# The second layer's last feed-forward product as seven half-width block products, under a planner that prices changes of the array's shape

## The chip, the cores and the metric

The kernel runs on one core of a Trainium2 chip. The metric is the device time of one launch in microseconds (us). Five engines work side by side, each on its own queue: TensorE (PE: matrix products, with its weight loads listed apart as PEld), VectorE (DVE), ScalarE (ACT), GpSimd (POOL) and SyncE (SP, which here only issues DMAs). Products land in eight PSUM banks of 512 fp32 columns; everything else lives in SBUF, 128 partitions wide.

## The reference

64 graphs of 256 nodes with 256 features, all in fp32, pass two layers. Layer 0 is two graph-attention steps and a feed-forward block; layer 1 is relational attention of eight heads and a feed-forward block:

```python
# layer 0
h = gat(gat(x, adj, W1, a1), adj, W2, a2)            # softmax over leaky_relu(Wh1 + Wh2^T), masked by adj
h = layernorm(x + h)
x = layernorm(h + relu(h @ w_ff1 + b_ff1) @ w_ff2 + b_ff2)         # 256 -> 1024 -> 256
# layer 1
attn = softmax(q @ k^T / sqrt(32))                    # 8 heads of 32 columns
out = sum over r of (attn * (adj == r)) @ v_r         # relations
x = layernorm(x + out @ Wo + bo)
x = layernorm(x + gelu(x @ W1 + b1) @ W2 + b2)        # W2 is 1024 x 256: the product that is changed
```

## The kernel before

**Units of work.** Graphs are taken in pairs; each of the 32 pairs passes `gat_layers`, `feed_forward` stage 0 (relu), `attention` (stage 1) and `feed_forward` stage 2 (gelu). Several pairs are in flight at once, in different stages (`run(..., 4)`).

**Matmuls.** Nearly every product goes through `by_strips` (L113): a 128-column stationary operand is cut into four strips of 32 columns, each of which writes its own 32 partitions of a bank, so the array works as four column strips. A call of `by_strips` is four matmuls in the program; each fp32 matmul is two `MATMUL` records in the trace, so a call is eight records. Below, "a group" is one such call. The scores of attention (L929) are different: they contract over 32 rows and work as four row strips; the trace writes their shape 32*128 and that of the others 128*32.

**Products by seven.** First products of the feed-forward and the q, k and v products already multiply 2x2 blocks by the seven-product scheme (class `Blocks`, steps `p1` to `p7`; `Second` makes the four sums of the right-hand blocks on VectorE, L402; L435 adds the bank to what is there).

**The second feed-forward product.** `by_eight` computes it plainly: for each graph g and half of its rows j, eight groups of 256 columns accumulate in a bank. That is 32 groups a pair and layer; nothing but the activations of `ff` and a free bank is waited for, so the planner spreads these groups as filling wherever nothing else is ready. `add_rows` (L617) then adds the bank to the residual rows and sums each row with the same instruction; `layernorm` goes on with the squares on ScalarE (L645), the root on GpSimd (L650, L651) and centre and scale on VectorE (L654, L657). The function `by_seven` is in the file and is not called, for `SEVEN = ()`.

**Order.** A planner in the program sets the order of every engine's queue before anything runs: `put` registers a piece of work for VectorE, ScalarE, GpSimd or SyncE with a duration, a rank and the events it needs; the generators `yield` what the next TensorE step needs; `run` keeps a clock for each engine, always serves the engine that can begin first, picks TensorE's step by `degree` (lowest first, then the oldest pair) among those ready for `SLACK` us, and other engines' pieces by rank. `free` counts the buffers (`x` and `adj` four, `ff` four blocks that only one pair may hold, PSUM banks eight). `alone` lets one pair at a time into each of "gat", "ff" and "attention". `keep_order` fixes the order found.

**Other names used below.** `transposed` turns rows on VectorE (`yb`, L678), stores them and gathers them back by DMA (`home`, `yT`); on five occasions at the head and tail (`hurried`) TensorE transposes instead (L709), with four strips of 32 columns and 128 moving columns. In attention `weight` takes the exponentials (L938), `mask` multiplies (`m`, L942), `halves` adds (`h`, L946), `products` multiplies with the values (L960, L963), `into_rows` with `Wo`. In the graph attention L551 scales the rows.

Of the kernel before, what the change touches and what calls it, by code (L numbers as in the profile page):

```python
# [15 lines left out]
ALU = mybir.AluOpType  # L16
# [11 lines left out]
SEVEN = ()  # L28
SLACK = 0.3
# [4 lines left out]
def two_layers(ctx: ExitStack, tc: tile.TileContext, t: dict, out: bass.AP, flag: bass.AP):  # L34
# [114 lines left out]
    alone, filling = {}, []  # L149
# [81 lines left out]
    def run(besides, ways, together):  # L231

        going, ways = [[besides, *next(besides)]], iter(ways)
        together += 1
        def degree(g):
            if g[0] in filling:
                return 2
            return 0 if "ff" in (g[2] or ()) or alone.get("ff") is g[0] else 1  # L240

        together += 1
        while True:
            while len(going) < together and (way := next(ways, None)) is not None:
                going.append([way, *next(way)])
            first = []
            for engine, pieces in waiting.items():
                times = [(at, n) for n, p in enumerate(pieces) if (at := begins(p["ready"], p["needs"])) is not None]
                if times:
                    first.append((max(min(times)[0], clock[engine]), engine, times))  # L250
            times = []
            for n, (way, events, name, banks, *more) in enumerate(going):
                if all(alone.get(n) in (None, way) for n in name or ()) and all(e.time is not None for e in events):
                    at = begins(max([e.time for e in events], default=0.0), "bank" if banks else None, banks)
                    for needs in more:
                        at = None if at is None else begins(at, needs)
                    if at is not None:
                        times.append((at, n))
            if times:
                first.append((max(min(times)[0], clock["tensor"]), "tensor", times))  # L260
            if not first:
                assert not going
                return
            now, engine, times = min(first)
            able = [n for at, n in times if at <= now]
            clock[engine] = now
            if engine == "tensor":
                sure = [n for at, n in times if at <= now - SLACK]
                g = going[min(sure, key=lambda n: (going[n][0] is besides, degree(going[n]), n))
                          if sure else min(times)[1]]  # L270
                alone.update((name, g[0]) for name in g[2] or ())
                takes("bank", g[3])
                for needs in g[4:]:
                    takes(needs)
                step = next(g[0], None)
                if step is None:
                    together -= g[0] is besides
                    going.remove(g)
                else:
                    g[1:] = step  # L280
            else:
                piece = waiting[engine].pop(min(able, key=lambda n: (waiting[engine][n]["rank"], waiting[engine][n]["first"]["ready"])))
                takes(piece["needs"])
                if piece["function"] and piece["function"] != table[0]:
                    table[0] = piece["function"]
                    clock[engine] += 1.3
                piece["emit"]()
                clock[engine] += piece["us"]
                end = clock[engine] + piece["lag"]
                if piece["kb"]:  # L290
                    moved[0] = max(moved[0], clock[engine]) + piece["kb"] / 380.0
                    end = moved[0] + piece["lag"]
                frees_at(end, piece["frees"])
                happens(piece["event"], end)
            keep_order()
# [8 lines left out]
    def load(pair, at=None):  # L304
# [29 lines left out]
        def in_bytes(there):  # L334
            return put("vector", 1.35, largest, put("scalar", 1.2, small_adj, there, needs="adj", rank=2), rank=2)
# [51 lines left out]
    class Second:  # L387


        def __init__(self, b, name, *events):  # L390
            self.b, self.name, self.there, self.read = b, name, [], []
            for n in range(3):
                self.there.append(put("vector", 0.34, lambda n=n: self.add(n), *events, rank=0, needs=None if n else name))
                events = self.there[-1:]
# [9 lines left out]
        def read_by_second(self, event):  # L404
            self.read.append(event)
            if len(self.read) == 2:
                put("vector", 0.34, lambda: self.add(3), self.there[2], *self.read, rank=0, event=self.there[3])
# [7 lines left out]
    class Blocks:  # L415
# [17 lines left out]
        def add(self, c, h, bank, *events, frees=()):  # L433
            def add():
                nc.vector.tensor_tensor(self.target(c, h), self.bank[bank], self.target(c, h), ALU.add)  # L435
            there = put("vector", 0.6, add, *events, rank=-1, frees=frees)
# [41 lines left out]
    def addends(y, there, at, layer, pair):  # L478
# [20 lines left out]
        there = put("scalar", 0.6, exps, *there, rank=0, function="exp")  # L499
# [28 lines left out]
        there = put("vector", 0.2, turn, there, rank=0)  # L528
# [3 lines left out]
    def gat_weights(y, at, at_home, ratio, there, to, b):  # L532
# [20 lines left out]
        there = put("vector", 0.95, lambda: weigh(0), *there, rank=b / 2, needs="e")  # L553
        there = put("vector", 1.13, lambda: weigh(1), there, rank=b / 2, frees=["rows"] * b)
        return of, put_each("scalar", 0.4, [lambda j=j: scale(j) for j in range(2)], there, rank=0)

    def gat_layers(pair, to, loads):
# [3 lines left out]
        def evacuated(to, k, wide, ps):  # L561
            return put("scalar", 0.3, lambda: nc.scalar.activation(to[:, k, :wide], ps[:, :wide], AF.Copy),
                       took(0.88), frees=["bank"])
# [45 lines left out]
    def add_rows(y, p, b, *events):  # L609
# [12 lines left out]
        return of, put_each("vector", 0.44, [lambda j=j: add(j) for j in range(2)], *events, frees=["bank"])  # L622

    def means(y, b, *events):
# [8 lines left out]
        return of, put_each("scalar", 0.54, [lambda j=j: mean(j) for j in range(2)], *events)  # L633

    def layernorm(r, gb, b, added, *events):
# [23 lines left out]
        there = put_each("scalar", 0.54, [lambda j=j: square(j) for j in range(2)], there, rank=0)  # L659
        centred = put_each("vector", 0.34, [lambda j=j: centre(j) for j in range(2)], there)  # L660
        there = put("gpsimd", 1.2, root, there, rank=0)
        return put_each("vector", 0.34, [lambda j=j: scale(j) for j in range(2)], there, centred, *events)
# [5 lines left out]
    def transposed(y, ready, to, b, pair, stage):  # L668
# [23 lines left out]
        there = put("vector", 0.62, turn, ready, needs="yb")  # L692
# [25 lines left out]
    def feed_forward(y, normal, w, func, relieved, gb, pair, stage):  # L718
# [11 lines left out]
        def slabs(t):  # L730
# [11 lines left out]
            def copy(c, h, event):  # L742
                return put("scalar", 0.5, lambda: nc.scalar.activation(target(c, h), blocks.bank["x"], AF.Copy), event, rank=-1)  # L743

            def activate(c, h, event, of=None, frees=()):
                for n in range(2):
# [3 lines left out]
                        to, source, func, bias=b1[:, m:m + 1]), event, rank=h - 1, function=kind,  # L750
# [9 lines left out]
        for step in (a.p1, b.p1, a.p2, a.p6, b.p2, b.p6, a.p5, a.p7, b.p7, b.p5, a.p4, b.p4, a.p3):  # L760
            yield from step()
# [28 lines left out]
    def by_seven(y, normal, f, evacuated, w2, w2_there, last):  # L790
# [21 lines left out]
        def add(to, of, us, *events, frees=()):  # L812
            return put("vector", us, lambda: nc.vector.tensor_tensor(to, of, to, ALU.add), *events, rank=-1, frees=frees)

        def combine(to, a, b, op, *events):
            return put("vector", 1.14, lambda: nc.vector.tensor_tensor(to, a, b, op), *events, rank=0)
# [40 lines left out]
    def attention(y, normal, pair, all_adj):  # L857
# [13 lines left out]
        there = put("scalar", 0.52, lambda: in_one_piece(0), normal[0], needs="yTa")  # L871
        there = put("scalar", 0.52, lambda: in_one_piece(1), there, normal[1], frees=["yT"])
# [27 lines left out]
        def with_bias_qk(c, b, event, frees=()):  # L900
            def copy(n):
                nc.scalar.activation(target_qk(c, b)[:, n], of_qk.bank["x"][:, n], AF.Identity, bias=bqk[:, n, c:c + 1])  # L902
            return [put("scalar", 0.4, lambda n=n: copy(n), event, rank=-1, frees=list(frees) * n) for n in range(2)][1]

        def with_bias_v(r, b, event, frees=()):
# [3 lines left out]
            return put("vector", 0.6, copy, event, rank=-1, frees=frees)  # L909
# [11 lines left out]
        def scores(n):  # L921
            b, c = divmod(n, KC)
            yield [ready["qk", c, b]], None, HQ
# [7 lines left out]
            there = took(1.13)  # L931
# [12 lines left out]
            def halves(q):  # L944
# [3 lines left out]
            there = [put_each("scalar", 0.48, [lambda q=q, k=k: weight(q, k) for k in range(2)], there, rank=0, function="exp",  # L948
                              needs="a", frees=["bank"] * 2) for q in range(HQ // 2)]
            masked.append([put("vector", 1.14, lambda q=q: mask(q), there[q], rank=0, needs="m") for q in range(HQ // 2)] +  # L950
                          [put("vector", 0.61, lambda q=q: halves(q), there[q], rank=0, needs="h") for q in range(HQ // 2)])

        def products(n):
# [10 lines left out]
            there = took(2.34)  # L964
# [16 lines left out]
            there = put("vector", 1.3, invert, there, rank=0)  # L981
            put("scalar", 0.4, check, there, rank=3)
            return put("vector", 0.34, lambda: nc.vector.tensor_tensor(to, po[:, :N], s, ALU.mult), there, rank=0, frees=["bank", "h"])
# [10 lines left out]
        a_, b_ = of_qk, of_v  # L994
        for step in (a_.p1, b_.p1, a_.p2, a_.p6, b_.p2, a_.p5, b_.p6, a_.p7, b_.p5, a_.p4, b_.p7, a_.p3, b_.p4, lambda: scores(0), b_.p3, lambda: scores(1)):
            yield from step()
        frees_at(clock["tensor"], ["yTa", "sums_yTa"])
        divided = []
        for n in range(4):
            yield [*masked[n], ready["v", 0, n // 2], ready["v", 1, n // 2]], None, 1  # L1000
            divided.append(products(n))
            if n < 2:
                yield from scores(n + 2)
# [85 lines left out]
    def whole_way(pair):  # L1089
        to, loads = loaded.pop(pair)  # L1090
        if pair + 1 < NPAIR and pair + 1 not in loaded:
# [5 lines left out]
        put("sync", 0.4, lambda: nc.sync.dma_start(  # L1097
            out[2 * pair:2 * pair + 2].rearrange("b (c p) d -> p (b c) d", p=P), to["x"]),
            normal[0], normal[1], rank=2, lag=1.8, kb=512, frees=["x"])

    run(reliefs(), (whole_way(pair) for pair in range(NPAIR)), 4)


# [442 lines left out]
```

## Time and profile before

| | before |
|---|---|
| median of 3 runs | 3002.74 us (3000.09 to 3004.53) |
| the profiled execution: time, span of its instructions | 3002.45 us, 3000.6 us |
| mean granted TensorE clock | 0.996 |
| PE busy, PE records | 2962.5 us (99%), 53778 |
| DVE busy | 2308.1 us (77%) |
| ACT busy | 1789.2 us (60%) |
| POOL busy | 293.3 us (10%) |
| HBM | 67 GB/s over the span |

Busy times are sums over the span; a busy PE is not a PE at its peak, since the ends of its matmuls are modelled, so the spacing of starts is what tells how fast it goes. A row of the groups reads: line, engine, operation, tiles written and read with their shapes, count, then busy time, the mean ns of one instruction, and the idle time ahead of them with what ended it. In a timeline a row reads: start, length, engine and line, what it writes and reads, and how many instructions were merged; two starts that follow each other give the rate.

### The profile page before, as it was taken

The page shows a single profiled execution, that of the slowest core. Times are in us where ns is not written, and L with a number is a line of the kernel's source. Part 1 is how long each engine was busy: PE and PEld are TensorE (multiplying, and loading weights), DVE is VectorE, ACT ScalarE, POOL GpSimd, SP SyncE. Part 2 cuts the span into 40 slices and gives each one's busy share as a digit, 9 for nine tenths or more (in the row PEclk, how much of TensorE's full clock was granted, in tenths as well). Part 3 has the DMA queues.
Part 4 walks back from the last instruction along what each step waited for, and adds up shares of the span by engine and source line. Part 5 has one row for each costly group of instructions (what it writes and reads, how often), then busy time and mean ns, then how long its engine had stood idle before and what let it go on. Part 6 is the DMA issues. An engine that isn't in the chain of part 4 may idle for free. (4 is left out here: it accounts for less than half of the span.)

```text
span 3000.6 us, 122479 instructions
## 1 busy us (share of the span) xinstructions
PE 2962.5 (99%) x53778; PEld 1766.1 (59%) x53778; DVE 2308.1 (77%) x5865; ACT 1789.2 (60%) x4644; POOL 293.3 (10%) x518
## 2 busy tenths in 40 slices
PE   7999999999999999999999999999999999999998
PEld 4655555555555555555555555555556555565665
DVE  5787875888668887588976888768886788867775
ACT  4555565665656566556665566555666565664554
POOL 0000010000101011000110001101010001100001
PEclk8999999999999999999999999999999999999999
DMA  5221231112321123121231212311232121321100
GB/s 178 80 72 52 65 110 63 52 59 66 108 65 55 55 72 119 52 69 38 92 103 55 62 51 89 99 52 59 65 97 76 59 65 53 100 74 49 39 10 24
DMA packets 211420, 210.22 MB, mean 70 GB/s; under 512 B 22336, under 2 KB 170432, under 8 KB 210880
## 3 DMA queue, kind: packets, MB, share of 16 engines
q1 hardware_dynamic: 210464, 202.06, 21.2%
q8 instruction: 424, 6.95, 1.0%
q14 instruction: 116, 0.95, 0.1%
q10 hardware_dynamic: 416, 0.26, 0.0%
HBM read 137.51 MB, written 64.73 MB: 67 GB/s over the span
## 5 line engine op out<-in xcount | busy, mean ns | idle before, releaser
L113 PE MATMUL ps<-w_L_gnn_W,ff 128*32 128x256 f32 x8192 | 470.7, 380 | 1.3 <-ACT ff L749 1.3
L113 PE MATMUL ps<-w_L_gnn_w_ff,ff 128*32 128x256 f32 x8192 | 470.7, 379 | 0.0
L113 PEld LDWEIGHTS ps<-w_L_gnn_W,ff 128*32 128x32 f32 x8192 | 260.1, 110 | 186.5 <-issue 13.6
L113 PEld LDWEIGHTS ps<-w_L_gnn_w_ff,ff 128*32 128x32 f32 x8192 | 265.1, 110 | 177.5 <-issue 3.6
L938 ACT ACTIVATE a<-ps 128x512 f32<-128x512 f32 x512 | 265.5, 600 | 170.3 <-PE ps L929 153.4
L435 DVE TENSOR_TENSOR ff<-ps,ff 128x512 f32<-128x512 f32 x384 | 262.3, 684 | 118.1 <-PE ps L113 89.6
L650 POOL TENSOR_SCALAR rstd<-squares 128x2 f32<-128x2 f32 x256 | 90.8, 355 | 2679.6 <-ACT unread L645 2678.3
L645 ACT ACTIVATE unread<-x,less 128x256 f32<-128x256 f32 x512 | 259.3, 506 | 130.1 <-DVE less L620 103.7
L942 DVE TENSOR_TENSOR m<-a,adj 128x1024 f32<-128x1024 f32 x256 | 310.7, 1214 | 23.9 <-ACT a L938 23.0
L113 PE MATMUL ps<-yT,w_L_gnn_W1p 128*32 128x256 f32 x5120 | 310.0, 379 | 0.8 <-ACT ff L743 0.3
L113 PE MATMUL ps<-yT,w_L_gnn_w_ff1p 128*32 128x256 f32 x5120 | 306.7, 379 | 0.0
L617 DVE SCALAR_TENSOR_TENSOR x<-ps,x 128x256 f32<-128x256 f32 x512 | 197.3, 417 | 136.0 <-PE ps L113 133.0
L743 ACT ACTIVATE ff<-ps 128x512 f32<-128x512 f32 x384 | 224.2, 588 | 112.9 <-PE ps L113 111.3
L113 PE MATMUL ps<-xw,e 128*32 128x258 f32 (+1 forms) x4096 | 242.7, 386 | 11.9 <-ACT xw L551 11.9
L551 ACT ACTIVATE xw<-xw,rs 128x258 f32<-128x258 f32 (+1 forms) x256 | 118.0, 504 | 201.2 <-DVE rs L547 201.1
L113 PEld LDWEIGHTS ps<-yT,w_L_gnn_W1p 128*32 128x32 f32 x5120 | 165.6, 110 | 112.9 <-ACT ff L743 4.9
L113 PEld LDWEIGHTS ps<-yT,w_L_gnn_w_ff1p 128*32 128x32 f32 x5120 | 165.5, 110 | 110.9 <-issue 2.3
L902 ACT ACTIVATE qk<-ps,bqk 128x256 f32<-128x256 f32 x256 | 107.1, 469 | 190.0 <-PE ps L113 189.8
L749 ACT ACTIVATE ff<-ff,c_L_gnn_b_ff 128x256 f32<-128x256 f32 x384 | 175.5, 503 | 50.5 <-DVE ff L435 47.8
L651 POOL TENSOR_TENSOR rstd<-rstd,mhalf 128x2 f32<-128x2 f32 x256 | 201.8, 788 | 21.3
L113 PEld LDWEIGHTS ps<-xw,e 128*32 128x32 f32 x4096 | 133.8, 112 | 104.6 <-ACT xw L551 14.1
L749 ACT ACTIVATE ff<-ff,c_L_gnn_b 128x256 f32<-128x256 f32 x384 | 175.9, 502 | 28.6 <-DVE ff L435 26.0
(126 smaller groups left out, 4748.2 us busy)
## 6 DMA issues: line engine op xcount, KB each, us to landing
home<-yb SPq DMA_DIRECT2D x182, 256.0 KB, 2.1
yT<-home SPq DMA_DIRECT2D x728, 64.0 KB, 2.1
rows<-row SPq DMA_DIRECT2D x60, 512.0 KB, 3.9
input<-in_xT SPq DMA_DIRECT2D x32, 512.0 KB, 4.0
x<-in_x SPq DMA_DIRECT2D x32, 512.0 KB, 3.9
out<-x SPq DMA_DIRECT2D x32, 512.0 KB, 3.0
input<-in_adjT SPq DMA_DIRECT2D x30, 512.0 KB, 4.0
v<-in_adjT SPq DMA_DIRECT2D x2, 512.0 KB, 7.5
```

What stands on the lines that cost most here:

```text
L113: nc.tensor.matmul(to[at:at + DH], lhsT=lhsT[:, at:at + DH], rhs=rhs, **flags)
L435: nc.vector.tensor_tensor(self.target(c, h), self.bank[bank], self.target(c, h), ALU.add)
L551: nc.scalar.activation(y[:, k, :at], y[:, k, :at], AF.Copy, scale=of["rs"][:, j:j + 1])
L617: nc.vector.scalar_tensor_tensor(row, p[:, j * D:(j + 1) * D], 1.0, row, op0=ALU.mult, op1=ALU.add, accum_out=of["less"][:, j:j + 1])
L645: nc.scalar.activation(unread, rows[j], AF.Square, bias=of["less"][:, j:j + 1], accum_out=squares[:, j:j + 1])
L650: nc.gpsimd.tensor_scalar(rstd, squares, 1.0 / D, EPS, ALU.mult, ALU.add)
L651: nc.gpsimd.tensor_tensor(rstd, rstd, mhalf[:, :2], ALU.pow)
L743: return put("scalar", 0.5, lambda: nc.scalar.activation(target(c, h), blocks.bank["x"], AF.Copy), event, rank=-1)
L749: evacuated[h][m] = put("scalar", 0.4, lambda m=m, to=to, source=source: nc.scalar.activation(to, source, func, bias=b1[:, m:m + 1]), even ...
L902: nc.scalar.activation(target_qk(c, b)[:, n], of_qk.bank["x"][:, n], AF.Identity, bias=bqk[:, n, c:c + 1])
L938: nc.scalar.activation(a[n][q][:, k], ps[2 * q + k], AF.Exp)
L942: nc.vector.tensor_tensor(m[n][q], a[n][q], adj, ALU.mult)
```

## The change

1. **By seven.** `SEVEN = (2,)`: the second product of stage 2 runs through `by_seven`. W2 is loaded by `last_weights` as seven blocks of 512 x 128 (four DMAs in place of one); `last_sums` makes three of them and rewrites a fourth with four VectorE subtractions at the start. Per pair seven products of eight groups with 128 moving columns take the place of 32 groups with 256. Between them VectorE makes four block sums of the activations (`combine`, t1 to t4, 128 x 1024 each, in place) and six additions of banks to the residual rows (d1, d5, d6, d3 of 128 x 256; d24 and d7 of 128 x 512). `add_rows` falls away in this stage; the row sums come from `means`, four ScalarE passes with an accumulator (L645 after, 128 x 256 each). The product order is 4, 1, last step of the first product, 5, 6, 2, 7, 3.
2. **The planner knows shapes.** A step may be named "rows" (the scores); a change between it and the others adds 0.1 to the planner's TensorE clock, the scores' and the products' own planned durations are lowered to match, and `degree` has a place for "rows" and for a second one in a row. `GROUPS` writes out how products and scores alternate.
3. **Five pairs** may be in flight (`FLIGHT = 5`), with the same buffers.
4. **Chosen precedences.** `SLACK` is 0; ranks of all kinds of pieces stand in `RANK`, the degrees in `DEGREE`, and the orders of the steps in `FIRST` (feed-forward) and `QKV` (attention).
5. The output of a pair is stored in two halves, each as soon as its graph is ready, where one DMA stored both.

```diff
-SEVEN = ()
-SLACK = 0.3
+SEVEN = (2,)
+SHAPES = ("rows",)
+SLACK = 0
+FLIGHT = 5
+RANK = {"adj": 1.5, "second": 0.5, "blocks": 0, "exps": 1.5, "addends": 1.5, "weigh": 3, "ratios": 0, ...
+DEGREE = {"first": 0.5, "gat": 1, "attention": 1.5, "fill": 2.5, "rows": -1, "after": 2.5}
+GROUPS = (([0], []), ([], [2]), ([1], []), ([], [3]), ([2], []), ([3], []))
+FIRST = ("a1", "a2", "b1", "a6", "b6", "b2", "a7", "a5", "b7", "a3", "b4", "a4", "b5")
+QKV = ("a1", "b1", "b2", "a6", "a2", "a5", "b6", "b7", "b5", "a7", "a4", "a3", "s0", "b4", "b3", "s1")
...
-            if g[0] in filling:
-                return 2
-            return 0 if "ff" in (g[2] or ()) or alone.get("ff") is g[0] else 1
+            kind = ("fill" if g[0] in filling else "first" if "ff" in (g[2] or ()) or alone.get("ff") is g[0] else
+                    "attention" if "attention" in (g[2] or ()) or alone.get("attention") is g[0] else "gat")
+            return DEGREE["after" if shaped[0] and shape(g) else shape(g) or kind]
...
+                if shape(g) != shaped[0]:
+                    clock[engine] += 0.1
+                    shaped[0] = shape(g)
...
-        centred = put_each("vector", 0.34, [lambda j=j: centre(j) for j in range(2)], there)
+        centred = put_each("vector", 0.4, [lambda j=j: centre(j) for j in range(2)], there, rank=RANK["centre"])
...
-            there = took(1.13)
+            there = took(0.97)
...
-            there = took(2.34)
+            there = took(2.17)
...
-        for n in range(4):
-            yield [*masked[n], ready["v", 0, n // 2], ready["v", 1, n // 2]], None, 1
-            divided.append(products(n))
-            if n < 2:
-                yield from scores(n + 2)
+        for groups, later in GROUPS:
+            yield from narrow(groups, later)
...
-        put("sync", 0.4, lambda: nc.sync.dma_start(
-            out[2 * pair:2 * pair + 2].rearrange("b (c p) d -> p (b c) d", p=P), to["x"]),
-            normal[0], normal[1], rank=2, lag=1.8, kb=512, frees=["x"])
+        there = []
+        for b in range(2):
+            there.append(put("sync", 0.4, lambda b=b: nc.sync.dma_start(
+                out[2 * pair + b].rearrange("(c p) d -> p c d", p=P), to["x"][:, of_graph(b), :]),
+                normal[b], *there, rank=2, lag=1.8, kb=256, frees=["x"] * b))
-    run(reliefs(), (whole_way(pair) for pair in range(NPAIR)), 4)
+    run(reliefs(), (whole_way(pair) for pair in range(NPAIR)), FLIGHT)
```

`by_seven`, which stood in the file and is called now (`done`, `quarter` and `two_halves` pick activations, a quarter of the rows and a bank):

```python
        def product(n, to, side, first=False):
            for b in range(2):
                for k in range(half):
                    by_strips(to[:, b], lhsT=side[:, k, b * P:(b + 1) * P], rhs=w2[:, n - 1, k], ...)
            return took(1.8)
        ...
        read4 = product(4, left[:, 0], a22, True)
        t1 = combine(a22, a21, a22, ALU.add, *done(0, 0), *done(0, 1), read4)
        t3 = combine(a21, a11, a21, ALU.subtract, *done(1, 1), t1)
        yield done(1, 1), None, 1
        read1 = product(1, x, a11, True)
        d1 = add(quarter(0, 0), x, 0.34, read1)
        t2 = combine(a11, a22, a11, ALU.subtract, t3, read1)
        yield from last.p3()
        ...
        yield [t1], None, 1
        read5 = product(5, v, a22, True)
        d5 = add(quarter(1, 1), v, 0.34, read5)
        yield [t2, d1], None, 0
        d6 = add(quarter(0, 1), x, 0.34, product(6, x, a11))
        yield done(1, 0), None, 0
        read2 = product(2, left[:, 1], a12)
        d24 = add(rows[:, :, :, :P], left, 0.6, read2, read4, frees=["bank"])
        t4 = combine(a12, a12, a11, ALU.subtract, t2, read2)
        yield [t3, d6], None, 0
        d7 = add(...product(7, x, a21), d5, frees=["bank"])
        yield [t4, d5], None, 0
        d3 = add(quarter(0, 1), v, 0.34, product(3, v, a12), frees=["bank"])
        normal["added"] = [means(y, g, d24, d7, d3) for g in range(2)]
```

## The prediction

> **What bounds the kernel now.** I first read the busy times of the page, then the same by stretches of the span:
>
> ```profile
> PE 2962.5 (99%) x53778; PEld 1766.1 (59%) x53778; DVE 2308.1 (77%) x5865; ACT 1789.2 (60%) x4644; POOL 293.3 (10%) x518
> ...
> 0.00:100.00 100.00, 80.67 (x1273) 52.36 (x1276) 57.54 (x185) 46.31 (x120) 5.15 (x14) 0.90 0.49 150
> 100.00:1000.00 900.00, 894.19 (x16236) 529.63 (x16232) 709.65 (x1805) 541.47 (x1423) 89.62 (x154) 1.00 0.23 70
> 1000.00:2000.00 1000.00, 997.74 (x18180) 593.26 (x18176) 776.02 (x1979) 611.74 (x1574) 102.29 (x181) 1.00 0.23 73
> 2000.00:2950.00 950.00, 948.82 (x17316) 565.55 (x17312) 744.58 (x1842) 571.86 (x1487) 89.94 (x160) 1.00 0.19 61
> 2950.00:3000.60 50.60, 41.08 (x798) 25.31 (x786) 20.29 (x57) 17.83 (x46) 6.27 (x11) 0.95 0.08 24
> ```
>
> After the length of each stretch come PE, PEld, DVE, ACT and POOL. From 100 to 2950 us PE has nothing to do for only 5.8 + 2.3 + 1.2 = 9.3 us; the rest of its 38 idle us lie in the first 100 us (19) and the tail (9.5). VectorE is at 78% there. So the time is PE's work plus head and tail. A busy share doesn't say how fast PE is; the timeline's starts do:
>
> ```profile
> 1573.64 12.27 PE L113 MATMUL ps<-w_L_gnn_W,ff 128*32 128x256 f32 x224
> 1585.73 2.77 PE L113 MATMUL ps<-yT,w_L_gnn_w_ff1p 128*32 128x256 f32 x48
> ...
> 1637.02 2.77 PE L113 MATMUL ps<-yT,w_L_gnn_w_ff1p 128*32 128x256 f32 x48
> 1639.72 1.15 PE L929 MATMUL ps<-qk 32*128 32x256 f32 x16
> 1640.80 1.07 PE L960 MATMUL ps<-a,v 128*32 128x256 f32 x16
> 1641.68 1.05 PE L960 MATMUL ps<-m,v 128*32 128x256 f32 x16
> ...
> 2952.88 1.06 PE L709 MATMUL ps<-ident,x 128*32 128x128 f32 x32
> 2953.75 1.91 PE L113 MATMUL ps<-w_L_gnn_W,ff 128*32 128x256 f32 x32
> 2955.48 1.06 PE L709 MATMUL ps<-ident,x 128*32 128x128 f32 x32
> 2956.35 1.03 PE L113 MATMUL ps<-w_L_gnn_W,ff 128*32 128x256 f32 x13
> ```
>
> The first two rows are the product to be replaced: 224 records in 12.09 us, so a group of eight takes 0.432 us. The last four hold the shape that replaces it (strips of 32, 128 moving columns): 32 records in 0.87 us, 0.218 us a group. Half the columns cost 50.5% of the time, in bursts. The middle rows price a change of shape: 48 records start 2.70 us ahead of the scores where six groups need 2.59; the scores hold PE 1.08 us where two groups need 0.86; the next 16 take 0.88. That is 0.11 + 0.22 + 0.02 = 0.35 us for going there and back.
>
> [...] the trace lists 110 ns a load, overlapping, and can't say whether they would hold a longer run back. [...]
>
> **The change, part by part.**
>
> *PE work.* Removed per pair: 32 groups x 0.432 = 13.82 us. Added: 7 x 8 = 56 groups x 0.218 = 12.21. Saved 1.61 us, over 32 pairs **-51 us**. Bounds: the best is this; if a product of eight groups takes the planner's 1.8 instead of 1.75, 7 x 0.05 x 32 = 11 us of it are lost.
>
> *Shape changes.* In the instruction order after, the scores are still 128 separate blocks of eight, never two in a row. The 128 x 0.35 = 45 us stay: **0**. Pricing them in the plan moves steps, it removes none.
>
> *VectorE.* Rows for the prices:
>
> ```profile
> L942 DVE TENSOR_TENSOR m<-a,adj 128x1024 f32<-128x1024 f32 x256 | 310.7, 1214 | 23.9 <-ACT a L938 23.0
> L435 DVE TENSOR_TENSOR ff<-ps,ff 128x512 f32<-128x512 f32 x384 | 262.3, 684 | 118.1 <-PE ps L113 89.6 <-ACT ff L743 27.1 <-ACT unread L645 0.5
> L617 DVE SCALAR_TENSOR_TENSOR x<-ps,x 128x256 f32<-128x256 f32 x512 | 197.3, 417 | 136.0 <-PE ps L113 133.0 <-PE ps L1111 2.3
> ```
>
> Added: 128 block sums x 1.214 = 155 us, 128 small adds x 0.415 = 53, 64 wide ones x 0.684 = 44. Removed: 128 row additions x (0.417 + 0.082 for reading the accumulator) = 64, and 64 small scalings x 0.169 = 11. Net +177 us: 2308 + 177 = 2485, 84% of the forecast span. It lies beside PE, except where a product waits for it.
>
> *The wait that is new.* `by_eight` waited for nothing behind its activations; five products of `by_seven` wait for VectorE. The order after is the same for nearly 27 pairs in a row, so one walk stands for most. Zero is the end of product 4. PE: `Wo` 1.73, product 1 to 3.48, last first-product step 0.86, so product 5 starts at 4.34, 6 at 6.09, 2 at 7.83, 7 at 9.58, 3 at 11.33. VectorE's order, each at its mean less the 0.08 us by which neighbours overlap (two of 476 ns last 0.88 in the tail's timeline), from 0.2: t1 to 1.33, a centre 1.73, t3 2.86, two row additions with their small scaling 3.86, t2 5.0, d1 5.3 (product 6 wants both at 6.09: 0.8 to spare), the last `ff` addition 5.9, a sum, a centre, d5, a sum 7.3, two scales 8.1, a sum, d6 8.8 (product 7 at 9.58: 0.8 to spare), `yb` 9.4, two centres 10.2, t4 11.35; [...]. So **+0.2 us a pair, +6 us**. Bounds: 0 if VectorE enters early, about 1 us a pair (+32) if it enters late, since all behind it is shifted.
>
> *ScalarE.* `means` add 128 x (0.506 + 0.190) = 89 us. In the order after, exponentials and gelu change places twice a pair, 64 table loads where the trace counts 53 + 35 + 17 + 1 = 106; 42 x 1.283 = 54 us go. Net +35: 61%, beside PE, which is busy throughout: **0** in the middle; with that cover gone it would be at most these 35 us. GpSimd makes the same 256 roots. Attention's exponentials no longer meet as many loads, which is why I cost their re-ordering at nothing.
>
> *Five pairs, ranks, orders.* They can win back at most the 9.3 us that PE idles between 100 and 2950, and lose what a badly placed wait costs. I take **0**; bounds -9 and +10. The `x` buffers stay four, so the fifth pair can run only to the end of its graph attention. The head (19 idle us, and 10 lost in two stretches at half clock, PEclk 0.90) is bound by the first loads; its order changes in details: **0**, bounds -8 and +8. Three more weight DMAs and four subtractions lie there, far ahead of their first use; 32 more output DMAs on SP, half as large, stand behind no load that PE awaits.
>
> *Tail.* Today one graph's normalization follows the last matmul. After, both wait for d3: d3 0.4, then four means and four squares on ScalarE at 0.61, 4.9 in all, where now two row additions and two squares take 2.2. **+3 us**; the last store is half as large, so between +1 and +5.
>
> *Sum:* -51 + 6 + 3 = -42 against the profiled execution's 3002.45, so 2960.4; the median of the runs is 0.3 above that execution: **2960**.
>
> **Rivals.**
>
> *VectorE becomes the second bound* (0.15): at 84% it enters the run of products about 0.7 us late in most pairs, behind attention's `m` and `h`; 22 us more, 2980 (2978 to 2996). For it: the walk leaves t4 no room. Against: in attention the order gives all masks of a block some 0.7 us or more before its product.
>
> *Slower* (0.08): the same place, carried further. PE has no filling between products 5 and 3, which stand together as 160 matmuls in the order, so each us that VectorE arrives late is paid in full. From 1.5 us late a pair the saving is eaten, from 1.7 the kernel is slower; at 2 us 2960 + 58 = 3018. Against: ranks put the block sums ahead of everything they meet.
>
> *No gain* (0.03): the short matmuls aren't sustained. If sets of four need 123 ns instead of 109 because their weight loads fall behind, 56 x 2 x 0.123 = 13.8 us, nothing is saved. [...] against: eight sets in a row kept 109.
>
> *More* (0.05): head and idle time shrink too: 2935.
>
> **How the numbers follow.** The likeliest case, 0.69, is 2960, own range 2940 to 2978 (bounds of head, tail, product rate and stall). Range 2938 to 2990, leaving out most of the case "more", the end of the second-bound case and the slower one. A measurement can tell about 0.2% (6 us) from no change: faster 0.69 + 0.15 + 0.05 = 0.89, same 0.03, slower 0.08.
>
> **What would show it.** PE records 53778 + 6144 = 59922; new matmuls of 128 columns at 0.218 us a group (1.75 a product); scores still 1.08; DVE near 2485 us; 64 table loads; idle PE ahead of products 6, 7 and 3 with a DVE releaser, near 0.2 us a pair. Wrong, if sets take over 115 ns, if PE waits over 1 us a pair for L828 or L831 (the changed kernel's additions and block sums), or if the idle between 100 us and the tail is over 40 us.

## The result, and the profile after

The change is faster by 1.5%: 2958.09 us median (2957.19 to 2962.04, 4 runs) against 3003.23 (3000.09 to 3004.53, 4 runs, one more than in the table above), a ratio of 0.9854 with a 95% interval of 0.9839 to 0.9868. The profiled execution took 2957.19 us, its span is 2955.4. The forecast was 2960, with a range of 2938 to 2990.

The same views as before, of the changed kernel: the page's busy times, then the stretches (length, PE, PEld, DVE, ACT, POOL, granted clock, DMA share, GB/s).

```profile
PE 2915.5 (99%) x59922; PEld 1908.3 (65%) x59922; DVE 2459.3 (83%) x5869; ACT 1796.1 (61%) x4858; POOL 266.3 (9%) x518
```

```profile
0.00:100.00 100.00, 77.66 (x1192) 49.29 (x1196) 58.15 (x183) 43.63 (x114) 4.85 (x14) 0.88 0.48 150
100.00:1000.00 900.00, 898.57 (x18327) 577.29 (x18320) 764.39 (x1842) 558.78 (x1518) 81.62 (x160) 1.00 0.23 74
1000.00:2000.00 1000.00, 1000.00 (x20640) 653.39 (x20636) 847.05 (x2024) 619.00 (x1678) 91.06 (x180) 1.00 0.23 73
2000.00:2900.00 900.00, 899.05 (x18675) 596.11 (x18671) 757.35 (x1750) 550.92 (x1479) 81.67 (x153) 1.00 0.19 61
2900.00:2955.40 55.40, 40.20 (x1118) 32.23 (x1110) 32.40 (x74) 23.80 (x70) 7.12 (x12) 0.91 0.07 23
```

PE is even fuller than before, with 1.4 + 0.0 + 1.0 = 2.4 us of idle between 100 and 2900 us; what has shrunk is its work. The timeline of one pair's seven products, TensorE alone (L122 is `by_strips`, which was L113):

```profile
1508.28 1.93 PE L122 MATMUL ps<-w_L_gnn_W,ff 128*32 128x128 f32 x64
1510.03 1.91 PE L122 MATMUL ps<-w_L_gnn_Wo,qk 128*32 128x256 f32 x32
1511.75 1.93 PE L122 MATMUL ps<-w_L_gnn_W,ff 128*32 128x128 f32 x64
1513.50 1.05 PE L122 MATMUL ps<-yT,w_L_gnn_W1p 128*32 128x256 f32 x16
1514.36 9.08 PE L122 MATMUL ps<-w_L_gnn_W,ff 128*32 128x128 f32 x320
1523.26 2.77 PE L122 MATMUL ps<-yT,w_L_gnn_w_ff1p 128*32 128x256 f32 x48
```

Product 4 holds PE from 1508.28 to 1510.03, 1.75 us, and product 1 the same. Products 5, 6, 2, 7 and 3 are the 320 records from 1514.36 to 1523.26: 8.90 us where five times 1.75 is 8.75. The missing 0.15 us is a wait that PE's idle time doesn't show, since the modelled ends of the matmuls cover it. The list of waits names it, in 27 pairs of 32 (waiting engine, who was waited for, us in total, times, longest):

```profile
PEld ps L122 <- DVE ff L831: 5.8, 27, 0.2
```

VectorE's timeline in the same stretch shows the four block sums (L831) and what stands ahead of the fourth:

```profile
1510.35 1.23 DVE L831 TENSOR_TENSOR ff<-ff 128x1024 f32<-128x1024 f32 x1 [0.20 <-ACT ff L763]
...
1511.88 1.22 DVE L831 TENSOR_TENSOR ff<-ff 128x1024 f32<-128x1024 f32 x1
...
1513.90 1.22 DVE L831 TENSOR_TENSOR ff<-ff 128x1024 f32<-128x1024 f32 x1
...
1518.83 0.71 DVE L692 STREAM_TRANSPOSE yb<-x 128x512 f32<-128x512 f32 x1
1519.45 0.84 DVE L668 SCALAR_TENSOR_TENSOR x<-x,less,b_L_gnn_g 128x256 f32<-128x256 f32 x2
1520.21 1.22 DVE L831 TENSOR_TENSOR ff<-ff 128x1024 f32<-128x1024 f32 x1
```

t4 ends 11.40 us after product 4 (1521.43 less 1510.03); product 3 could have started at 1514.36 + 4 x 1.75 = 1521.36. The groups that are new (busy time, mean ns, idle time ahead), and ScalarE's new pass and most of its table loads, which in the trace stand ahead of a gelu and of an exponential in turn (five more stand at other lines, 64 in all):

```profile
L831 DVE TENSOR_TENSOR ff<-ff 128x1024 f32<-128x1024 f32 x128 | 156.1, 1220 | 10.1 <-ACT ff L763 6.1 <-PE ps L122 3.7
L828 DVE TENSOR_TENSOR x<-ps,x 128x256 f32<-128x256 f32 x128 | 53.3, 417 | 3.5 <-PE ps L122 2.7 <-PE ps L1135 0.8
L828 DVE TENSOR_TENSOR x<-ps,x 128x512 f32<-128x512 f32 x64 | 44.0, 688 | 4.1 <-PE ps L122 1.0
```

```profile
L645 ACT ACTIVATE unread<-x 128x256 f32<-128x256 f32 x128 | 53.4, 417 | 44.7 <-DVE x L828 41.9 <-DVE all_of_them L1137 0.2
L763 ACT ACT_TABLE_LOAD x32 | 41.1, 1283 | 0.6
L508 ACT ACT_TABLE_LOAD x27 | 34.6, 1283 | 0.1
```

### The profile page after: what moved, and what is told of

The parts are those of the page before. It is cut to its first block, busy times and chain, and to the rows that moved or that the text cites. A ratio compares the mean times of both kernels' runs of the same rounds, so it can differ in the third digit from the quotient of the medians.

```text
span 2955.4 us, 135318 instructions
## 1 busy us (share of the span) xinstructions
PE 2915.5 (99%) x59922; PEld 1908.3 (65%) x59922; DVE 2459.3 (83%) x5869; ACT 1796.1 (61%) x4858; POOL 266.3 (9%) x518
## 4 chain that ended last, share of the span: by engine, by line
## 5 line engine op out<-in xcount | busy, mean ns | idle before, releaser
L122 PE MATMUL ps<-w_L_gnn_w_ff,ff 128*32 128x256 f32 x8192 | 490.4, 380 | 0.0
L122 PE MATMUL ps<-w_L_gnn_W,ff 128*32 128x128 f32 x14336 | 414.5, 273 | 0.3 <-issue 0.3
L122 PEld LDWEIGHTS ps<-w_L_gnn_W,ff 128*32 128x32 f32 x14336 | 393.8, 110 | 23.3 <-DVE ff L831 5.8
L122 PEld LDWEIGHTS ps<-w_L_gnn_w_ff,ff 128*32 128x32 f32 x8192 | 259.7, 110 | 187.3 <-issue 30.2
L122 PE MATMUL ps<-yT,w_L_gnn_W1p 128*32 128x256 f32 x5120 | 307.8, 381 | 4.6 <-ACT yT L727 4.0
L122 PE MATMUL ps<-yT,w_L_gnn_w_ff1p 128*32 128x256 f32 x5120 | 306.1, 379 | 0.5 <-DVE ff L449 0.4
L664 POOL TENSOR_SCALAR rstd<-squares 128x2 f32<-128x2 f32 x256 | 61.3, 240 | 2661.7 <-ACT unread L659 2661.5
L122 PE MATMUL ps<-xw,e 128*32 128x258 f32 (+1 forms) x4096 | 245.3, 386 | 13.3 <-ACT xw L565 13.2
L122 PEld LDWEIGHTS ps<-yT,w_L_gnn_W1p 128*32 128x32 f32 x5120 | 166.1, 110 | 111.0 <-ACT yT L727 4.2
L122 PEld LDWEIGHTS ps<-yT,w_L_gnn_w_ff1p 128*32 128x32 f32 x5120 | 168.5, 110 | 103.2 <-DVE ff L449 0.9
L631 DVE SCALAR_TENSOR_TENSOR x<-ps,x 128x256 f32<-128x256 f32 x384 | 145.1, 414 | 74.7 <-PE ps L122 74.4
L665 POOL TENSOR_TENSOR rstd<-rstd,mhalf 128x2 f32<-128x2 f32 x256 | 204.3, 798 | 21.3
L122 PEld LDWEIGHTS ps<-xw,e 128*32 128x32 f32 x4096 | 136.0, 112 | 103.8 <-ACT xw L565 16.4
L960 DVE TENSOR_TENSOR h<-a 128x512 f32<-128x512 f32 x256 | 167.8, 687 | 15.3 <-ACT a L952 15.3
L122 PE MATMUL ps<-yTa,wqk 128*32 128x256 f32 x2560 | 167.2, 379 | 0.2 <-DVE qk L449 0.2
```

What stands on the lines that cost most here:

```text
L122: nc.tensor.matmul(to[at:at + DH], lhsT=lhsT[:, at:at + DH], rhs=rhs, **flags)
L631: nc.vector.scalar_tensor_tensor(row, p[:, j * D:(j + 1) * D], 1.0, row, op0=ALU.mult, op1=ALU.add, accum_out=of["less"][:, j:j + 1])
L664: nc.gpsimd.tensor_scalar(rstd, squares, 1.0 / D, EPS, ALU.mult, ALU.add)
L665: nc.gpsimd.tensor_tensor(rstd, rstd, mhalf[:, :2], ALU.pow)
L960: nc.vector.tensor_tensor(h[n][q], a[n][q][:, :, :N], a[n][q][:, :, N:], ALU.add)
```

## The experiments

In the table, "idle" is PE's idle time between 100 and 2900 us: 2800 less its busy time there, from the stretches of each run's trace. Short waits are hidden in busy time, so "lost" counts otherwise: every record of TensorE in that stretch at the start-to-start price that unbroken stretches of its shape show in the traces of before and the change (27.3 ns for 128 columns, 54.0 for 256, 54.4 and 54.8 for 258 and 260, 67.3 in the scores), taken from 2800. Some 16 us of it are changes of shape (128 times 0.13, the 0.11 and 0.02 of the timeline before; the rest of their price being in the scores' 67.3). As the prices are rounded, "lost" may be off by a few us; its differences are better.

Each ratio below is to runs of the kernel before that were made beside the experiment; their medians lie between 3003.4 and 3004.7 us. A difference to the change, whose runs were made at another time, can be off by 1 or 2 us.

| kernel | median us | idle us | lost us |
|---|---|---|---|
| before | 3003.2 | 9.3 | 31 |
| the change | 2958.1 | 2.4 | 25 |
| plain product, all else changed (e1) | 3016.9 | 21.1 | 45 |
| seven products, nothing else (e2) | 3037.1 | 55.5 | 100 |
| the change with four pairs (e3) | 3011.2 | 32.3 | 74 |
| the change without shapes (e4) | 2970.9 | 11.6 | 34 |
| one more VectorE operation ahead of t4 (e5) | 2991.7 | 34.3 | 56 |
| the same operation behind d24 (e6) | 2959.5 | 3.6 | 26 |
| product planned at 1.75 us (e7) | 2953.6 | 3.5 | 22 |
| seven products in both layers (e8) | 3008.4 | 55.8 | 126 |
| before, seven products and five pairs (e9) | 3035.7 | 58.9 | 103 |
| before, five pairs (e10) | 3026.2 | 21.3 | 46 |
| e7 with six pairs (e11) | 2968.8 | 14.3 | 38 |
| the change with the old ranks (e12) | 2999.1 | 39.0 | 71 |

### Which part of the change brings the time

**e1**, the new plan without the products:

```diff
-SEVEN = (2,)
+SEVEN = ()
```

> The changed kernel with the plain second product in both layers, so the new planner, five pairs and precedences alone. Theory (the seven products are the gain): TensorE's work is that of before again, so about 50 us more than the change less the 6 us of waits and the 3 us of tail, 2958 + 41 = 2999, within 9 us of before (2990 to 3004). Rival (the better plan brought most of it): under 2980, since the order alone would have won 25 us or more.

3016.85 us (3016.74 to 3019.99), ratio to before 1.005 (1.0033 to 1.0066). Both theories missed: the plan alone isn't neutral, it is slower than before. TensorE waits for q and k once in nearly every pair (PE's own waits):

```profile
PE ps L122 <- DVE qk L449: 16.5, 27, 1.6
```

An order that fits the changed work doesn't fit the old. An order chosen for the plain product was not looked for. In the middle it could win at most some 15 us: the 31 lost before, less the 16 of the shapes.

**e2**, the products without the new plan:

```diff
-SEVEN = ()
+SEVEN = (2,)
```

> The kernel before with the seven products in the second layer and nothing else changed. Theory (TensorE's work sets the time, the plan only has to keep up): 2955 to 2975, that is nearly the whole gain. Rival (the seven products only pay under the new plan, since under the old one TensorE waits for VectorE between them): 2985 or more, with over 20 us of TensorE idle behind VectorE's block sums and additions.

3037.13 us (3034.47 to 3038.96), ratio 1.0111 (1.0094 to 1.0128). My theory fell and the rival held. TensorE has the same work as in the change, and what it loses more than eats the gain: 100 us in the middle where it was 31 before, and some 16 us more at the tail. The longest waits of its weight loads for another engine:

```profile
PEld ps L113 <- DVE ff L816: 37.3, 34, 2.6
PEld ps L113 <- ACT ff L743: 25.1, 29, 2.2
```

One pair in its timeline, TensorE:

```profile
1462.01 3.68 PE L113 MATMUL ps<-w_L_gnn_W,ff 128*32 128x128 f32 x128
1465.50 1.05 PE L113 MATMUL ps<-yT,w_L_gnn_W1p 128*32 128x256 f32 x16
1466.66 1.95 PE L113 MATMUL ps<-w_L_gnn_W,ff 128*32 128x128 f32 x64
1470.59 5.45 PE L113 MATMUL ps<-w_L_gnn_W,ff 128*32 128x128 f32 x192 [1.97 <-DVE ff L816]
1476.23 1.96 PE L113 MATMUL ps<-w_L_gnn_W,ff 128*32 128x128 f32 x64 [0.20 <-DVE ff L816]
```

Products 4 and 1 stand together as 128 records, without the `Wo` block that lies between them in the change. So product 5 comes due 1.73 us sooner after product 4 and waits for t1; product 5 ends at 1466.66 + 1.75 = 1468.41 and product 6 starts at 1470.59, over 2 us late, behind t3 and t2. VectorE is also late to begin: t1 starts at 1465.39, 1.63 us after product 4 (1462.01 + 1.75 = 1463.76), where in the change it starts 0.32 us after it (1510.35 less 1510.03).

**e9**, the products and the fifth pair under the old precedences (`SEVEN = (2,)`, and 5 for 4 in `run`):

> The kernel before with the seven products in the second layer and five pairs in flight, all precedences as before. Theory (the seven products need both, a fifth pair and an order in which VectorE serves them in time): 2985 to 3030, with TensorE still waiting 25 us or more for VectorE ahead of the products. Rival (the fifth pair alone makes them pay, as the loss with four suggests): 2975 or less.

3035.65 us (3030.53 to 3046.24), ratio 1.0106 (1.0079 to 1.0134). The fifth pair doesn't rescue the products; the time is over the theory's range, too. The waits behind the block sums shrink to 10.7 us for the weight loads (37.3 in e2) and 6.1 for the matmuls behind them, below the 25 I expected, and others take their place: weight loads wait 38.7 us for `ff` from ScalarE (25.1 in e2).

**e10**, the fifth pair alone:

> The kernel before with five pairs in flight and nothing else. Theory (with the plain products as filling TensorE idles only 9 us in the middle, so there is nothing for a fifth pair to fill): 2994 to 3012. Rival (a fifth pair is worth as much here as in the changed kernel, where taking it away cost 53 us): under 2980.

3026.18 us (3025.64 to 3035.05), ratio 1.008 (1.006 to 1.01). Slower than either theory said: 15 us more lost in the middle, 9 at the tail, and nothing at the head.

**e3**, four pairs (`FLIGHT = 4`) in the changed kernel:

> The changed kernel with four pairs in flight. Theory (TensorE never lacks work between head and tail, a fifth pair adds nothing): 2955 to 2966. Rival (with less filling the fifth pair is what keeps TensorE supplied): 2975 or more, with idle TensorE in the middle of the span.

3011.24 us (3008.61 to 3023.92), ratio 1.0033 (1.002 to 1.0045). The rival held: 53 us lost, with 32.3 us of idle, spread over the graph attention's products (weight loads wait 32.5 us for L565), the `ff` blocks (22.2) and the masks (16.5).

**e12**, the old ranks in the changed kernel:

```diff
-RANK = {"adj": 1.5, "second": 0.5, "blocks": 0, ... "sums": -1, "qk": -2, ... "mask": 1, ... "centre": 2, ...}
+RANK = {"adj": 2, "second": 0, "blocks": -1, ... "sums": 0, "qk": -1, ... "mask": 0, ... "centre": 1, ...}
```

> The changed kernel with the ranks of all pieces as they were before (block sums of the second product and masks at 0, additions and bank copies at -1, the rest as in the kernel before); five pairs, degrees, the orders of the steps, the groups and the shape charge as changed. Theory (the ranks are what keeps VectorE and ScalarE ahead of TensorE): 2985 or more, TensorE idle over 30 us in the middle. Rival (step orders and degrees carry it, ranks are trimming): under 2972.

2999.14 us (2992.98 to 3006.6), ratio 0.9984 (0.9977 to 0.9991). The theory held: 41 us of the 45 go with the ranks alone. The wait that the change has at 0.2 us is here about 1 us in 29 pairs, seen by the weight loads (the matmuls behind them wait 19.9 us of it). It is about half of what is lost more in the middle; the rest is spread over other waits:

```profile
PEld ps L122 <- DVE ff L831: 27.7, 29, 1.3
```

**e4**, the planner without shapes (no charge, `took(1.13)` and `took(2.34)` as before, no degree for the scores):

> The changed kernel whose planner doesn't know the shape changes: no charge for them, the scores' and products' planned durations as before, the scores with no degree of their own; the rest as changed. Theory: the 128 changes of shape and their 0.35 us stay in both kernels, so it is within 10 us of the change (2952 to 2970). Rival (the pricing itself brings time): slower by 15 us or more.

2970.86 us (2969.0 to 2976.55), ratio 0.9896 (0.9879 to 0.9912). 12.8 us slower than the change, between the two theories. The scores are 128 blocks in each, and in the change's trace they still go from 1561.42 to 1562.50, 1.08 us, as before. So what the planner's better clock brings is not in the shapes; most of it is the wait for the block sums, which in the change comes to 5.8 us:

```profile
PEld ps L122 <- DVE ff L831: 17.3, 28, 1.1
```

### Where VectorE binds

**e5** and **e6** add the same operation of 1.2 us to each pair, unknown to the planner, in two places. **e5**, ahead of t4:

```diff
+    idle = const.tile([P, 4, N], F32, name="idle")
+    nc.vector.memset(idle, 0.0)
...
+        def late():
+            nc.vector.tensor_tensor(idle, idle, idle, ALU.add)
+            nc.vector.tensor_tensor(a12, a12, a11, ALU.subtract)
-        t4 = combine(a12, a12, a11, ALU.subtract, t2, read2)
+        t4 = put("vector", 1.14, late, t2, read2, rank=RANK["sums"])
```

> The changed kernel with one more VectorE operation a pair, a 128x1024 addition on a tile of its own, directly ahead of the block sum t4; the planner doesn't know of it, so every queue keeps its order. Theory (VectorE has no room left ahead of product 3, which has no filling behind it): product 3 waits 1.13 us longer in nearly every pair, 30 to 38 us more, 2988 to 2996. Rival (VectorE at 83% takes another 1.2% in its stride): under 2966.

2991.66 us (2989.04 to 2994.05), ratio 0.9961 (0.9946 to 0.9976): 33.6 us more than the change, as the theory said. TensorE shows it where it was expected, ahead of product 3 (L124 is the changed kernel's L122, L867 is t4):

```profile
1529.74 7.17 PE L124 MATMUL ps<-w_L_gnn_W,ff 128*32 128x128 f32 x256
1538.00 1.95 PE L124 MATMUL ps<-w_L_gnn_W,ff 128*32 128x128 f32 x64 [1.08 <-DVE ff L867]
```

Product 3 was due at 1529.74 + 4 x 1.75 = 1536.74 and starts 1.26 us later, where the change has 0.15. The 1.11 us between them in each of the 29 pairs that wait are 32 us.

**e6** (`idle` as in e5):

```diff
+        def both():
+            nc.vector.tensor_tensor(rows[:, :, :, :P], left, rows[:, :, :, :P], ALU.add)
+            nc.vector.tensor_tensor(idle, idle, idle, ALU.add)
-        d24 = add(rows[:, :, :, :P], left, 0.6, read2, read4, frees=["bank"])
+        d24 = put("vector", 0.6, both, read2, read4, rank=RANK["last"], frees=["bank"])
```

> The same additional operation, but two places later on VectorE, behind the addition d24, the planner again not knowing of it. Theory (it is the place and not the load that counts: no product stands behind it before VectorE has caught up): 0 to 8 us more, 2956 to 2966. Rival (VectorE is a second bound by its load): as much as with the operation ahead of t4, 25 us or more.

2959.52 us (2957.19 to 2959.97), ratio 0.9852 (0.9837 to 0.9867): nothing that these runs resolve. VectorE's busy time is the same in both (2496.6 and 2493.5 us), so it is the place and not the load: two operations further on, 32 operations of 1.2 us are free. The wait for t4 stays what it is in the change:

```profile
PEld ps L124 <- DVE ff L833: 5.8, 27, 0.2
```

**e7** sets the planner's figure to the measured one:

```diff
-            return took(1.8)
+            return took(1.75)
```

> The changed kernel with one figure of the planner set to what the trace shows: a product of eight half-width groups takes 1.75 us, not 1.8. TensorE's order in the steady stretch stays as it is; on VectorE one of the two centre operations that stood ahead of t4 falls behind it, so t4 ends 0.4 us earlier. Theory (product 3 waits about 0.2 us for t4 in 27 of 32 pairs): this wait goes, 4 to 7 us less, 2951 to 2955. Rival (the 0.2 us are a hand-over that stays whatever stands ahead): within 2 us of the change.

2953.61 us (2952.8 to 2956.63), ratio to before 0.9835 (0.9822 to 0.9848), 4.5 us better than the change; the runs of the two don't overlap, though the intervals of their ratios overlap a little. The five products go from 1512.41 to 1521.14, 8.73 us, and of the waits for L831 a single one of 0.3 us is left:

```profile
1512.41 8.92 PE L122 MATMUL ps<-w_L_gnn_W,ff 128*32 128x128 f32 x320
1521.14 2.77 PE L122 MATMUL ps<-yT,w_L_gnn_w_ff1p 128*32 128x256 f32 x48
```

This is the fastest version of the study.

**e8**, both layers (`SEVEN = (0, 2)`):

> The changed kernel with the seven products in both layers. TensorE's work falls by another 50 us, VectorE's rises by 177 to some 2640 us. Theory (no plain product is left as filling, VectorE is at 90%, and waits for it eat the gain): 2970 to 3040, over 60 us of TensorE idle more. Rival (TensorE's work still sets the time): under 2925.

3008.39 us (2997.97 to 3016.2), ratio 1.0014 (1.0006 to 1.0022). The time is in the theory's range, with 53 us more idle than the change where the theory had over 60. TensorE has 66066 records and waits most of all behind attention's masks on VectorE, which now is busy 2629.9 us (87%), and ScalarE 2034.8:

```profile
PEld ps L974 <- DVE m L956: 44.5, 49, 1.0
```

The ranks weren't chosen for this work, and the order that the planner finds here has 218 table loads of 1.28 us where the change has 64, so how much is VectorE's load and how much the order isn't told apart.

**e11**, six pairs on top of e7 (`FLIGHT = 6`):

> The changed kernel with the product's planned duration at 1.75 us, as in the run before, and six pairs in flight. Theory (TensorE idles under 4 us between head and tail, the sixth pair finds nothing to fill and the rows' buffers are four): 2950 to 2960. Rival (any other number of pairs than the one for which the precedences were chosen loses): 2970 or more, with TensorE idle in the middle.

2968.81 us (2963.93 to 2972.43), ratio 0.988 (0.9863 to 0.9896): 15 us worse than e7, just short of the rival's figure, with 14.3 us of idle, weight loads waiting 18.2 us for `ff` from ScalarE.

## Why the prediction was right, and where it wasn't

**PE work, -51: right.** A product takes 1.75 us alone, and 8.73 for five in e7, where nothing is waited for: 0.218 us a group over 320 records, as the transposes showed over 32. All records at their start-to-start prices come to 51 us less. The rival of short matmuls that can't be sustained is out: a set of four takes 109 ns in the long run, too (8.73 us over 80 sets), beside weight loads that the trace lists at 110 ns each, overlapping.

**The wait, +6: right.** The walk had product 3 due at 11.33 and t4 end at 11.35, and t4 ended at 11.40, step by step within 0.2 us of the walk. What the forecast of 0.2 us a pair held beyond these 0.02 was the author's estimate of a hand-over that no trace showed; here the first weight load of product 3 starts 0.05 us behind the end of t4 (1521.48 less 1521.43). In 30 pairs the five products stand together; beyond 8.73 us they lose 5.3 us in all, 0.16 in nearly every pair. Taking the cause away in e7 gave back 4.5 us. e5 tests the slope that the "slower" rival rested on, at one point: an operation that takes VectorE 1.13 us (from the start of t4 to that of the next in the change, 1520.21 to 1521.34) cost 1.11.

**Tail, +3: smaller where it was put, and a second part was missing.** From the end of the last product to the end of the span it was 3000.6 - 2991.07 = 9.5 us and is 2955.4 - 2944.2 = 11.2: +1.7. The prediction had all four means wait for d3; but d3 writes only one of the two blocks of rows that each graph has, and two of the means start ahead of it, at 2943.54 and 2944.08 against 2944.26. What it didn't have lies ahead of the last products: TensorE waits 4.0 us once for the last pair's transposed rows, and the 48 records behind that wait take 4.30 us in place of 2.59, at a granted clock of 0.60. Both together are +5.7.

**Head, 0: missed by 4,** within its bounds: 3 us more idle, and a granted clock of 0.88 for 0.90.

**Five pairs, ranks, orders, 0 within -9 and +10: this step failed,** though the sum didn't show it, in two ways. As a number: between 100 and 2900 us TensorE loses 6 us less than before in spite of the new waits of 5.3, so the rest has shrunk by 11. The bound was drawn from idle time alone, which leaves short waits out: weight loads waited 13.9 + 6.2 us for `ff` from ScalarE before, and 0.7 in the change. As an argument: it treated the plan as an addition to the products. The runs show that they can't be added. Against the kernel before, the products under the old plan cost 34 us, the fifth pair alone 22, both together 31, and the plan without the products 13; all of it wins 45. Taken from the whole, the ranks are worth 41 us, the fifth pair 53, the shapes 13. That the order can win back at most the idle of before could hold at best for a kernel whose products wait for nothing. Each of these settings makes the planner find another order, so the differences belong to that order and not to the setting as such; which ranks matter was not tried.

**Together** -51 + 5 + 7 + 4 - 11 = -46, where the spans differ by 45. PE's work and the wait came out as forecast, because they were walked through the order that the changed kernel really has. That the sum came within 2 us is in part luck: tail and head cost 9 us more than forecast, and the order gave 11 more.

**VectorE, +177:** the new groups took 156 + 53 + 44, as priced. The durations of all its instructions add up to 185 us more; the busy time rose by only 151, since the page counts overlapping neighbours once. **ScalarE, +35:** 64 table loads, as forecast. The pass of `means` was mis-sized: 417 ns and not the 506 of the squares, so 128 x (0.417 + 0.187) = 77 for 89. All durations add up to 30 us more, and the busy time, again for the overlaps, to 7 more.

**Rivals.** The late VectorE that "VectorE becomes the second bound" and "slower" rest on is what e2, e12 and e5 show; the change escapes it with 0.2 us a pair to the bad. Of "more", the idle time in the middle did shrink, by 7 us, and that of the head grew by 3.

## What to carry to other kernels

When filling that waits for nothing is replaced by less work that waits, the saving is only as good as the order: count the saved work, then walk the actual queue of the engine that feeds it through one period, with start-to-start prices, and see what stands ahead of each wait. Where the walk left no room, an operation of 1.13 us cost 1.11 a pair (e5); two places later it cost nothing that these runs resolve (e6). Parts that were fitted to each other can't be priced by undoing them one at a time; and of those that were tried alone here (the products, the fifth pair, the plan) none was worth keeping alone.

## What I had not expected of the hardware

The scores with their change of shape cost the same in both kernels: 1.07 to 1.08 us a block in 127 of the 128 blocks before and in all 128 after. Behind the one wait of 4.0 us at the tail TensorE's granted clock was 0.60 over 4.3 us, and wait and slow records together cost 5.7; whether the wait brought the lower clock was not tried. A ScalarE pass with an accumulator took 417 ns without a bias column and 507 with one, for 256 columns; the two also evaluate different functions, so the bias isn't shown to be the cause. And the activation behind a table load started 1.295 us after the load did, in the median of the change's 64; 42 fewer of these loads, at 1.283 us each, took 54 us off ScalarE.
